# A planner's price for matmuls, halved, in a kernel that weaves a second stream of work between scans

## The chip, the cores and the metric

The kernel runs on one core of a Trainium2 chip. The metric is the device time of one execution in microseconds (us), as the median of several runs.

## The reference

Four images of 96 channels and 64 x 64 pixels go through four layers, all in float32:

- Layer 0 is a state-space layer. After a layer norm, a projection to 192 channels, a 3 x 3 depthwise convolution and SiLU, the 4096 pixels are scanned in four directions (rows, columns, and both backwards) by `h = h * exp(dt * A) + dt * B * x`, `y = sum over 16 states of h * C`, for each of the 192 channels and 16 states. The sum of the directions is normalised, gated with SiLU of a second projection and projected back. An MLP with GELU follows.
- Layer 1 is a group norm, a 3 x 3 convolution and a scan with one state in two directions, gated.
- Layer 2 is a Fourier transform over the pixels with a pointwise complex step and the inverse transform, and an MLP whose operands are rounded to 8-bit floats.
- Layer 3 is a linear attention over 6 heads and a second 8-bit MLP.

## The kernel before

The scans of layer 0 are most of the work. `scan` runs over 4 images x 4 directions x 4 chunks of 1024 pixels x 24 tiles, 1536 tiles in all; a tile is 128 rows (32 channels x 4 states) by 1024 pixels. For each tile:

- GpSimd multiplies u by B into `w` (L745), 2.36 us; there are 9 w buffers.
- ScalarE makes the decay `h = exp(dt * A)` (L144), 1.12 us, with two h buffers, two tiles ahead.
- VectorE scans (L821), 2.35 us.
- The result is multiplied by C, on VectorE (L829, 1.22 us) for two tiles of three or so, on GpSimd (L841, 2.35 us) for the rest.
- The last column is kept as the state for the next chunk (L837 on ScalarE, L834 on GpSimd).
- TensorE sums the states of each two tiles (L767, `py`), three tiles later, and VectorE adds the sums to y (L779, L782).

All the rest is a second piece of work, the **stream**: Python generators whose steps are emitted between the scan's tiles. `front(b)` makes dt, u, B and C of an image (layer norm `pcen`, `pvar`; convolution `pc`; projections `px`, `pd`). `rest(b)` takes an image from the scan's result to the end: `tail` (`pz`, `pca`, `pcb`, `pv`, `po`, `ph`, `pm`), `l1`, `transform`, `middle` and `back`. The four fronts come first in the stream; `rest(b)` is added when image b's last direction begins, and its tail can begin a block of 1024 pixels once the scan has written that block. What is left after the scan is emitted four tasks abreast.

The order on each engine is the order in which the program is emitted. It is set by a planner: a clock for each engine, `now[e]`, and the end of the latest thing that depends on others, `chain[e]`. Each emitted operation adds an estimate to its engine's clock, not before the operands' estimated ends (`spend`, `tick`). For the stream's matmuls the estimate is made in `mm`. The scan's own operations have their fixed prices (sums: 1.5 us for two tiles). Twice a tile, `advance` decides whether the next step of the stream is emitted:

```
late = max(chain["pe"] - 0.5, now["act"], now["pool"] - 6.0, now["pe"] - 2.0) - free
if not put_off and late <= slack:
    step()
```

`free` is VectorE's clock after the scan (and 1.2 us more if VectorE also multiplies), with a slack of 2 us, and the clock 2.4 us on after the tile's end, with a slack of 1 us. VectorE's operations of the stream are not emitted at once: `later` puts them off with the time at which their operands should be there, the largest of the chains of TensorE, ScalarE and GpSimd, and `flush` emits them when VectorE's clock has come to it. While any is put off, no step is let out.

After the scan, steps alternate with a `flush()` that emits everything put off, so that no estimate decides the order there.

Of the kernel before, what the change touches and what calls it, by code (L numbers as in the profile page):

```python
# [11 lines left out]
F32 = mybir.dt.float32  # L12
# [44 lines left out]
def tile_hybrid(ctx: ExitStack, tc: tile.TileContext, I: dict, out: bass.AP):  # L57
# [8 lines left out]
    def tick(e, us, *behind):  # L66
        now[e] = max(now[e], 0.0, *behind) + us
        return now[e]

    def blocks(ap):  # L70
        t = ap.tensor
        if ap.space == DRAM:
            return []
        span = sum(abs(st) * (n - 1) for st, n in list(ap.ap)[1:])
        lo = ap.offset % int(np.prod(t.shape[1:]))
        return [(t.name, q) for q in range(lo // 512, (lo + span) // 512 + 1)]

    def spend(e, us, reads=(), writes=()):
        behind = [chain["dve"]]
        for ap in reads:  # L80
            behind += [done_at.get(q, 0.0) for q in blocks(ap)]
        for ap in writes:
            behind.append(used.get(slot_of.get(ap.tensor.name), 0.0))
        chain[e] = end = tick(e, us, *behind)
        for ap in writes:
            for q in blocks(ap):
                done_at[q] = end
        for ap in (*reads, *writes):
            if ap.tensor.name in slot_of:
                used[slot_of[ap.tensor.name]] = end  # L90

    def size(ap):
        return int(np.prod(ap.shape[1:]))

    def mm(o, lhsT, rhs, side=1, **kw):

        spend("pe", size(rhs) / side * (2.4e-3 if rhs.dtype == F32 else 1.2e-3), (lhsT, rhs), (o,))
        nc.tensor.matmul(o, lhsT=lhsT, rhs=rhs, **kw)  # L98

    dve = nc.vector  # L100
# [158 lines left out]
    def setup():  # L259
# [11 lines left out]
        pool.tensor_scalar(wx[rC], wraw, V("g1", rC), None, ALU.mult)  # L271
        pf = bank("pf")
        mm(pf[C : C + 1, 0:DI], lhsT=V("b1", rC), rhs=wraw, start=True, stop=True)
        dve.tensor_add(wx[C : C + 1], pf[C : C + 1, 0:DI], bi[C : C + 1])

# [18 lines left out]
    def weights():  # L294
# [8 lines left out]
        def task():  # L303
# [14 lines left out]
            pf = bank("pf")  # L318
            b1 = V("b1", rC)
            mm(pf[:, 0:1], lhsT=wraw[:, 0:128], rhs=b1, start=True, stop=True)  # L320
            for h in (lo64, hi64):
                mm(pf[h, 1:2], lhsT=wraw[:, 128:192], rhs=b1, start=True, stop=True)
# [1385 lines left out]
```

## Time and profile before

| | |
|---|---|
| median of 3 runs | 6824.64 us (6809.26 to 6828.71) |
| profiled execution | 6833.64 us, span 6831.9 us |
| instructions in the profile | 52664, of them 15538 matmuls |
| before the first scan | 97 us |
| the scan of 4 images | 97 to 6231 us |
| after the scan | 601 us |
| mean granted TensorE clock | 0.743 |

In the page, PE is TensorE, PEld its weight loads, DVE VectorE, ACT ScalarE and POOL GpSimd. A row of the page gives the line, engine and operation, what is written and read, the shapes, the count, the busy time, the mean of one in ns, and the engine's idle time before it with what ended most of it. A line of helpers stands for many operations: L98 is the matmul in `mm`, L144 the activation in `act`, L148 the copy. The tile names tell them apart.

### The profile page before, as it was taken

To read this page: it belongs to the slowest core of one execution; us is meant where nothing else is said; L and a number is where in the kernel's file an instruction comes from. 1 tells how busy PE (TensorE), PEld (TensorE's weight loads), DVE (VectorE), ACT (ScalarE), POOL (GpSimd) and SP (SyncE) were. 2 spreads that over 40 slices of the span, in tenths; PEclk is the share of its full clock that TensorE was granted. 3 is DMA by queue.
4 is the path that set the end of the run, shared out by engine and by line. 5 is a ranking of instruction groups with operands and counts; after the bars stand their busy time and mean duration, and the time that the engine had idled before them with its cause. 6 is when DMAs were issued, how large, how long until landed. Compare 5 with 4: busy or idle time off the path is not lost. (4 is left out here: it accounts for less than half of the span.)

```text
span 6831.9 us, 52664 instructions
## 1 busy us (share of the span) xinstructions
PE 4673.5 (68%) x15538; PEld 1514.0 (22%) x15538; DVE 5603.1 (82%) x3872; ACT 3731.0 (55%) x5242; POOL 5188.9 (76%) x2732
## 2 busy tenths in 40 slices
PE   6758667676677666666776675657676666576877
PEld 2112111121112124211111142211111332111353
DVE  3888779797789998998899998898999989984413
ACT  3556546666555545665555455566555456553337
POOL 4888879899779788998688898897887889972000
PEclk8768677686778778766777786668777876676987
DMA  5766666767544348444443375454434563442141
GB/s 149 217 194 193 185 180 192 208 207 210 156 132 143 116 136 262 137 146 144 134 151 125 98 262 155 131 158 139 143 128 127 189 209 127 133 144 83 43 125 37
DMA packets 502464, 1050.00 MB, mean 154 GB/s; under 512 B 138448, under 2 KB 252178, under 8 KB 501144
## 3 DMA queue, kind: packets, MB, share of 16 engines
q1 hardware_dynamic: 502176, 1046.63, 49.5%
q8 instruction: 123, 2.02, 0.1%
q14 instruction: 165, 1.35, 0.1%
HBM read 831.15 MB, written 211.09 MB: 153 GB/s over the span
## 5 line engine op out<-in xcount | busy, mean ns | idle before, releaser
L745 POOL TENSOR_TENSOR w<-u,bb 128x1024 f32<-128x1024 f32 x1536 | 3587.5, 2358 | 179.5 <-PE py L767 123.8
L144 ACT ACTIVATE h<-dt,negA 128x1024 f32<-128x1024 f32 x1536 | 1706.8, 1117 | 795.6 <-DVE w L829 429.2
L821 DVE TENSOR_TENSOR_SCAN h<-h,state,w 128x1024 f32<-128x1024 f32 x804 | 1886.8, 2347 | 271.9 <-ACT h L144 202.8
L829 DVE TENSOR_TENSOR w<-h,cc 128x1024 f32<-128x1024 f32 x1072 | 1309.0, 1221 | 56.7 <-DMA cc<-bc_d 18.8
L767 PE MATMUL py<-w,idup 128*32 128x512 f32 x6144 | 1125.3, 805 | 244.1 <-POOL w L841 80.9
L841 POOL TENSOR_TENSOR w<-w,cc 128x1024 f32<-128x1024 f32 x464 | 1092.0, 2353 | 188.3 <-DVE w L821 142.4
L821 DVE TENSOR_TENSOR_SCAN w<-h,state,w 128x1024 f32<-128x1024 f32 x348 | 814.5, 2341 | 50.9 <-ACT h L144 29.2
L837 ACT COPY state<-h 128x1 f32<-128x1 f32 x804 | 127.5, 159 | 1279.4 <-DVE w L829 1278.6
L821 DVE TENSOR_TENSOR_SCAN h<-h,w 128x1024 f32<-128x1024 f32 x268 | 612.9, 2287 | 103.6 <-ACT h L144 73.5
L98 PE MATMUL pc<-xp 97*64 97x512 f32 (+1 forms) x1152 | 400.2, 611 | 12.4 <-DMA xp<-wc_d 7.8
L767 PEld LDWEIGHTS py<-w,idup 128*32 128x32 f32 x6144 | 164.5, 126 | 1057.3 <-issue 597.3
L834 POOL COPY state<-w 128x1 f32<-128x1 f32 x348 | 64.3, 185 | 363.9 <-DVE w L821 363.1
L111 POOL TENSOR_TENSOR u<-dt,xi 128x512 f32<-128x512 f32 x160 | 216.8, 1371 | 156.7 <-ACT dt L144 142.3
L821 DVE TENSOR_TENSOR_SCAN w<-h,w 128x1024 f32<-128x1024 f32 x116 | 264.4, 2279 | 71.9 <-POOL w L745 55.1
L98 PE MATMUL pc<-xp,wc 96*96 96x512 f32 x576 | 275.1, 631 | 25.6 <-ACT u L144 25.6
L98 PE MATMUL pd<-xd,dtw 6*64 6x512 f32 (+1 forms) x512 | 211.4, 983 | 92.8 <-ACT xd L148 59.1
L98 PE MATMUL pcen<-t,cen 96*96 96x512 f32 x192 | 137.5, 853 | 161.3 <-POOL t L1332 78.8
L144 ACT ACT_TABLE_LOAD x176 | 225.8, 1283 | 32.0 <-PE pd L98 18.1
L136 ACT ACT_TABLE_LOAD x174 | 223.2, 1283 | 3.8 <-PEq L1698 0.7
L98 PEld LDWEIGHTS pc<-xp 97*64 97x64 f32 (+1 forms) x1152 | 149.9, 167 | 270.2 <-issue 239.4
L98 PE MATMUL po<-hq,q 128*96 128x512 fp8e5 x192 | 88.7, 586 | 163.0 <-POOL hq L1320 132.1
L98 PE MATMUL pvar<-sq,avg 96*96 96x512 f32 x256 | 168.9, 801 | 45.3 <-ACT sq L144 45.3
(242 smaller groups left out, 6330.8 us busy)
## 6 DMA issues: line engine op xcount, KB each, us to landing
u<-u_d SPq DMA_DIRECT2D x384, 512.0 KB
dt<-dt_d SPq DMA_DIRECT2D x384, 512.0 KB
bb<-bc_d SPq DMA_DIRECT2D x256, 512.0 KB
cc<-bc_d SPq DMA_DIRECT2D x256, 512.0 KB
dt_d<-dt SPq DMA_DIRECT2D x128, 256.0 KB
u_d<-u SPq DMA_DIRECT2D x128, 256.0 KB
f_d<-fo SPq DMA_DIRECT2D x64, 384.0 KB
a<-f_d SPq DMA_DIRECT2D x64, 384.0 KB
```

Source lines behind the costliest of these rows:

```text
L98: nc.tensor.matmul(o, lhsT=lhsT, rhs=rhs, **kw)
L111: aside(0.2 + size(o) * 2.1e-3, o, a, b).tensor_mul(o, a, b)
L136: nc.scalar.preload_act_table_set("natural_log_exp_and_others")
L144: nc.scalar.activation(o, i, func, **kw)
L745: pool.tensor_mul(w, us[ci, 2 * p + a], bbs[ci, g])
L767: nc.tensor.matmul(o, lhsT=idup, rhs=v, **flags)
L821: dve.tensor_tensor_scan(o[:, r], h[:, r], w[:, r], state if step else 0.0, ALU.mult, ALU.add)
L829: dve.tensor_mul(w, o, cc)
L834: pool.tensor_copy(state, o[:, last : last + 1])
L837: nc.scalar.copy(state, o[:, last : last + 1])
L841: pool.tensor_mul(w, o, cc)
```

## The change

The two factors of the estimate in `mm`, in us for each column of the moving operand: from 2.4e-3 to 1.2e-3 for float32, and from 1.2e-3 to 0.9e-3 for the other type that it is called with (8-bit floats). `side` is the number of such matmuls that are taken to run side by side. The operations stay the same; the order in which the stream's steps stand among the scan's tiles is worked out anew.

```diff
     def mm(o, lhsT, rhs, side=1, **kw):
 
-        spend("pe", size(rhs) / side * (2.4e-3 if rhs.dtype == F32 else 1.2e-3), (lhsT, rhs), (o,))
+        spend("pe", size(rhs) / side * (1.2e-3 if rhs.dtype == F32 else 0.9e-3), (lhsT, rhs), (o,))
         nc.tensor.matmul(o, lhsT=lhsT, rhs=rhs, **kw)
```

## The prediction

> **What bounds the kernel now.** I read the page's busy line first, then a table of windows (one for each image's scan, cut at the 1st, 385th, 769th and 1153rd scan instruction), then the waits, then single stretches of the timeline.
>
> ```profile
> span 6831.9 us, 52664 instructions
> ...
> PE 4673.5 (68%) x15538; PEld 1514.0 (22%) x15538; DVE 5603.1 (82%) x3872; ACT 3731.0 (55%) x5242; POOL 5188.9 (76%) x2732
> ...
> L98 PE MATMUL pc<-xp 97*64 97x512 f32 (+1 forms) x1152 | 400.2, 611 | 12.4 <-DMA xp<-wc_d 7.8
> ```
>
> Busy time, in the same order of engines as on the page, then the granted clock and the DMA share:
>
> ```profile
> 97.00:1641.00 1544.00, 1105.32 (x3438) 297.23 (x3439) 1301.14 (x787) 895.51 (x1197) 1325.45 (x713) 0.73 0.66 198
> 1641.00:3158.00 1517.00, 996.67 (x3399) 316.51 (x3397) 1369.41 (x930) 839.07 (x1173) 1294.82 (x675) 0.73 0.49 155
> 3158.00:4707.00 1549.00, 1047.23 (x3487) 332.36 (x3488) 1383.24 (x954) 854.14 (x1201) 1284.77 (x664) 0.74 0.48 152
> 4707.00:6231.00 1524.00, 1023.52 (x3476) 328.67 (x3474) 1378.74 (x948) 852.62 (x1195) 1266.71 (x656) 0.74 0.45 143
> 6231.00:6831.90 600.90, 457.14 (x1622) 224.00 (x1622) 166.63 (x244) 265.69 (x443) 1.55 (x8) 0.80 0.27 76
> ```
>
> The scan takes 6134 us of the span, and in it VectorE is busy 1301.14 + 1369.41 + 1383.24 + 1378.74 = 5432.53 us. It does the same instructions whatever the order, so the only thing that a new order can change there is VectorE's 701 us of idle time (11%). The last 601 us hold the rest of image 3, where every step is emitted with a flush of all put-off work and no estimate is asked: I give the change nothing there, within 15 us either way for how much of image 3's tail is already done.
>
> The waits in the scan (who <- whom: us in total, times, longest):
>
> ```profile
> ACT sbb L144 <- PE pcb L98: 62.4, 14, 7.0
> ACT y L148 <- PE py L98: 60.1, 20, 8.2
> ACT xd L148 <- PE px L98: 56.1, 14, 14.2
> ACT pvar L144 <- PE pvar L98: 52.6, 74, 2.9
> ACT sq L144 <- PE pcen L98: 50.0, 39, 7.8
> ```
>
> With the smaller rows of the same list, ScalarE stands 534 us in 392 waits for a matmul of the stream. VectorE's own rows: 396 us ended by ScalarE (decay, state), 131 us by the sums of line 767, 106 us by GpSimd. GpSimd in turn stands 124 us for line 767, which frees its w buffers. The tie between them is seen in one stretch of image 1's scan, in which the rest of image 0 runs:
>
> ```profile
> 1824.14 1.97 PE L98 MATMUL pcb<-ya,cenr 128*64 128x512 f32 x2
> 1826.04 1.97 PE L98 MATMUL pcb<-yb,cenr 64*64 64x512 f32 x2
> 1827.93 1.93 PE L767 MATMUL py<-w,idup 128*32 128x512 f32 x8
> 1828.04 0.60 ACT L144 ACTIVATE sbb<-pcb 128x512 f32<-128x512 f32 x1 [6.99 <-PE pcb L98]
> 1830.72 2.36 DVE L821 TENSOR_TENSOR_SCAN h<-h,state,w 128x1024 f32<-128x1024 f32 x1 [7.24 <-ACT state L837]
> ```
>
> ScalarE was given sbb too early, stood 6.99 us for TensorE, had the next decay and the state copy behind it, and VectorE lost 7.24 us.
>
> **What an estimate should be.** The six-call steps of pc call mm 36 times a task, 16 tasks: 576 calls. The page counts 1152 instructions. So one float32 mm is two instructions, and the 611 ns of the pc row is half a call. The back-to-back pace is in the timeline after the scan:
>
> ```profile
> 6337.55 61.98 PE L98 MATMUL pc<-xp,wc 96*96 96x512 f32 x144
> ```
>
> 61.98/144 = 0.43 us an instruction, 0.86 us a call, when TensorE is kept busy. The two pcb lines above show 1.97 us for two instructions, one call, when it is not. The old estimate for 512 columns is 512 x 2.4e-3 = 1.23 us, between the two. The new one, 0.61 us, is 0.7 of the fastest call and under a third of the slowest. For a conv step of six calls (5.2 us at 0.86 us a call) the old estimate, 7.4 us, was 2.2 us long and the new, 3.7 us, is 1.5 us short: a draw. For a two-call step of a layer norm or a projection (four instructions of 0.43 to 0.98 us: 1.7 to 3.9 us) the old 2.46 us lay inside and the new 1.23 us lies below.
>
> **What the Trainium skill says.** "TensorE: Matmul & The Clock Gate", part 1 (What's actually happening): the array runs at half rate until it has been busy for a window of about 3.4 us. The trace agrees: 0.43 against 0.98 us an instruction, mean granted clock 0.73 to 0.74 in the scan. The same page, Engine queue depths: ScalarE, VectorE and GpSimd take their queues strictly in order. The sbb stretch shows that for ScalarE. "Perfetto Trace Analysis" (Identifying the Most-Contended Engine) warns that matmul busy time misleads because matmuls are pipelined; hence the spacing is used above, not the 611 ns.
>
> **The change part by part.** No instruction is added or removed; the f8 matmuls' estimate goes from 0.61 to 0.46 us (0.75 times), float32 to a half. What moves is where the stream's steps stand between the scan's tiles.
>
> *The gate.* A step is let out when chain pe - 0.5, act, pool - 6 and pe - 2 are all within 2 (or 1) us of VectorE's clock. With a half as long estimate the pe terms, and act through what it reads, fall by 1.23 us for a two-call step and up to 3.7 us for a conv step. There are two chances a tile, 1.2 to 2.4 us apart, so the fall means about one chance earlier, where pe was what refused. Nothing waits for the stream to be ahead: the tails of images 1 and 2 start (first pz by its tile view at 3163 and 4596 us) while or just after the scan of that image ends (3158, 4707 us). So being earlier buys nothing in itself, and it leaves stretches with no step at the end of each image.
>
> *ScalarE.* An activation that reads a matmul now stands in its queue earlier. I let half of the 392 waits grow by the cut of a two-call step: 196 x 1.23 = 241 us. What of it reaches VectorE: against 534 us of such waits stand 396 us of VectorE's waits for ScalarE, which table loads and long activations cause too; I take 0.4. That makes +96 us. Bounds: 0.1 (the decay runs two tiles ahead and covers most) to 0.75 (the two sums' ratio): +24 to +180 us.
>
> *Behind it on other queues.* The stream's matmuls also stand earlier before the sums of line 767, and whatever TensorE has too much of delays py, the w buffers and GpSimd (131 + 106 us of VectorE's idle now). The put-off VectorE steps fall due by the same clocks and may then wait on VectorE itself (now 13 us, xr <- po). The stream's DMAs go with their steps on SP's one queue; image 0's scan, where all fronts run, moves 198 GB/s at share 0.66, and closer steps would raise it. Together I price these at +10 us, with -20 to +60 us as bounds.
>
> *Given back.* Closer matmuls may keep the clock up. If that takes a fifth off the 534 us, at the same 0.4, it is -43 us; bounds 0 and -110 us (half of it).
>
> Sum: 96 + 10 - 43 = **+63 us**. The profiled execution took 6833.64 us (span 6831.9 and 1.7 around it), 9.0 us over the median of 6824.64: 6897 us in its terms, **6888 us** as a median.
>
> **The rivals.** *Faster: the clock.* Steps let out closer together keep TensorE at full rate, and the waits shrink: in the tail at 3252 us, where two pcb instructions take 1.07 us in place of 1.97, sbb waits 3.4 us in place of 7.0. If 534 us of ScalarE's waits fall by a third, 178 us, at the same 0.4, that is -71 us: 6754 us. For it: clock 0.73 in the scan, so about half the time at half rate. Against it: tails and layer norms are chains, and a chain's matmuls are apart however early they are issued. It decides if the scan's mean clock rises over 0.80.
>
> *Nothing to be seen.* Other terms hold the step: in image 0 GpSimd's clock, later the put-off VectorE work, which refuses a step by itself. Then the steps hardly move: 6825 us.
>
> *It does not do what it says.* The trace's time may have been read per instruction, not per call: then the new estimate is no nearer to the chip than the old. That is part of the first case, and gives its sign.
>
> **How the numbers follow.** Slower as worked out: 0.50; its own range is 6845 us, where a loss can first be told, to 6995 us (180 for ScalarE, 10, -43 and some 20 us of chance). Faster through the clock: 0.37. No change: 0.13. Which stall meets which tile is partly chance: alike stretches now differ (VectorE idle in the four images' scans: 243, 148, 166, 145 us). The range over all cases goes down to 6730 us, the faster case and 25 us of that chance. A difference under 0.3% (20 us) is what this measurement cannot tell from none.
>
> **What would show it.** Right: VectorE's idle time in the scan over 730 us, ScalarE's waits for the stream's matmuls over 600 us in sum (now 534), fronts ended before 1640 us and the first pz before 1734 us, the last 601 us unchanged, the instruction counts the same. Wrong: those waits at or under 534 us, or the granted clock over 0.80. Then the estimate was too long for the chip, however many instructions a call has.

## Result: slower by 5.9%

The changed kernel takes 7224.32 us (7209.95 to 7243.31), the kernel before 6826.68 us beside it: a ratio of 1.059 [1.0558, 1.0621], 398 us (the bracket is a 95% interval, here and below). The forecast had the direction, to which it gave one chance in two; its +63 us is a sixth of the size, and the result lies above its range.

The page after, in the lines that answer to those of before:

```profile
span 7228.6 us, 52744 instructions
...
PE 4828.1 (67%) x15538; PEld 1532.5 (21%) x15538; DVE 5612.2 (78%) x3872; ACT 3749.8 (52%) x5245; POOL 5187.5 (72%) x2732
```

The matmuls (15538) and VectorE's instructions (3872) are the same in number; ScalarE loads its function table three times more (353 for 350). VectorE's busy time grew by 9 us. The windows by image, in the same columns as before:

```profile
98.00:1868.00 1770.00, 1275.73 (x3694) 338.59 (x3694) 1333.16 (x832) 987.71 (x1321) 1351.94 (x729) 0.72 0.62 182
1868.00:3446.00 1578.00, 1010.01 (x3371) 317.59 (x3374) 1370.52 (x931) 823.77 (x1149) 1274.70 (x661) 0.71 0.44 143
3446.00:5026.00 1580.00, 1013.75 (x3368) 316.43 (x3366) 1369.29 (x929) 823.44 (x1148) 1274.80 (x660) 0.70 0.45 143
5026.00:6622.00 1596.00, 1022.78 (x3368) 319.29 (x3368) 1368.58 (x929) 823.81 (x1148) 1268.51 (x658) 0.70 0.43 137
6622.00:7228.60 606.60, 462.03 (x1622) 225.12 (x1622) 166.47 (x243) 266.60 (x443) 1.55 (x8) 0.79 0.26 75
```

The part after the scan is as it was (607 against 601 us). The loss is in the scan, and there in VectorE's idle time: 6524 - 5442 = 1082 us, against 701 us. Image 0's scan, where the fronts run, is 226 us longer, the other three 61, 31 and 72 us. Some 32 us of image 0's share are no loss but VectorE's own work, which now falls into it (1333 us busy in place of 1301); its idle time there grew by 194 us, that of the others by 186 us together. The granted clock in the scan went down, from between 0.73 and 0.74 to between 0.70 and 0.72. The stream did get ahead: the last front matmul ends at 1532 us in place of 1696, and the first pz is at 1564 us in place of 1734.

The waits of the scan after (who <- whom: total, times, longest):

```profile
DVE h L821 <- ACT h L144: 394.9, 131, 18.4
...
POOL w L745 <- PE py L767: 357.9, 95, 13.9
...
DVE h L821 <- ACT state L837: 116.3, 58, 16.3
...
DVE w L821 <- ACT h L144: 104.7, 32, 11.0
```

The same four rows before:

```profile
DVE h L821 <- ACT h L144: 276.2, 144, 13.5
...
POOL w L745 <- PE py L767: 123.8, 57, 6.3
...
DVE h L821 <- ACT state L837: 44.2, 26, 7.2
...
DVE w L821 <- ACT h L144: 33.0, 17, 7.1
```

And from ScalarE's own list after:

```profile
ACT sbb L144 <- PE pcb L98: 86.8, 15, 7.0
ACT xi L144 <- PE pc L98: 79.4, 17, 8.9
...
ACT u L144 <- PE pc L98: 34.0, 15, 3.7
```

The two rows that name pc were not in the list of before at all. Taken over all rows, ScalarE stood 868 us for matmuls of the stream (552 before, the smallest rows included), VectorE's idle time ended by ScalarE went from 418 to 702 us, and GpSimd's waits for the sums from 124 to 358 us. Sorted by what ended it, VectorE's 381 us of new idle time are: ScalarE +284 us, TensorE +110 us (the sums +62, matmuls of the stream that VectorE reads itself +48), DMA +23 us, GpSimd -38 us. So GpSimd's longer waits for the sums do not show as waits of VectorE for GpSimd. In the 358 us for which GpSimd waited for the sums, TensorE was idle for only some 16 us (the two engines' instructions laid over each other): the sums stood behind other matmuls, not behind one that waited for its operand.

One stretch of the timeline, the conv steps of one task in image 0's scan, shows how the queues hang together:

```profile
540.69 7.96 PE L98 MATMUL pc<-xp 97*64 97x512 f32 x36
540.86 4.69 POOL L745 TENSOR_TENSOR w<-u,bb 128x1024 f32<-128x1024 f32 x2 [1.66 <-PE py L767]
...
548.58 1.07 PE L767 MATMUL py<-w,idup 128*32 128x512 f32 x8
548.70 0.69 ACT L144 ACTIVATE xi<-pc,vec 128x512 f32<-128x512 f32 x1 [8.21 <-PE pc L98]
...
549.74 2.35 POOL L745 TENSOR_TENSOR w<-u,bb 128x1024 f32<-128x1024 f32 x1 [4.19 <-PE py L767]
...
550.70 1.12 ACT L144 ACTIVATE h<-dt,negA 128x1024 f32<-128x1024 f32 x1
...
551.92 2.29 DVE L821 TENSOR_TENSOR_SCAN w<-h,w 128x1024 f32<-128x1024 f32 x1 [8.45 <-ACT h L144]
```

The 18 calls of pc2 stand in one piece between two sums. They take 7.96 us. The new estimate for them, with side 2, is 18 x 0.61 / 2 = 5.5 us, the old one 11 us. ScalarE came to SiLU 8.2 us too early, the decay stood behind it, the sums behind the matmuls, GpSimd behind the sums, and VectorE lost 8.45 us.

### The profile page after: what moved, and what is told of

The parts are those of the page before. It is cut to its first block, busy times and chain, and to the rows that moved or that the text cites. A ratio compares the mean times of both kernels' runs of the same rounds, so it can differ in the third digit from the quotient of the medians.

```text
span 7228.6 us, 52744 instructions
## 1 busy us (share of the span) xinstructions
PE 4828.1 (67%) x15538; PEld 1532.5 (21%) x15538; DVE 5612.2 (78%) x3872; ACT 3749.8 (52%) x5245; POOL 5187.5 (72%) x2732
## 5 line engine op out<-in xcount | busy, mean ns | idle before, releaser
L767 PE MATMUL py<-w,idup 128*32 128x512 f32 x6144 | 1278.5, 854 | 727.3 <-DVE y L782 268.2
L829 DVE TENSOR_TENSOR w<-h,cc 128x1024 f32<-128x1024 f32 x1072 | 1309.6, 1222 | 85.5 <-DMA cc<-bc_d 44.5
L767 PEld LDWEIGHTS py<-w,idup 128*32 128x32 f32 x6144 | 181.3, 129 | 1720.6 <-issue 602.3
L98 PE MATMUL pc<-xp,wc 96*96 96x512 f32 x576 | 252.5, 595 | 0.0
```

Source lines behind the costliest of these rows:

```text
L767: nc.tensor.matmul(o, lhsT=idup, rhs=v, **flags)
L829: dve.tensor_mul(w, o, cc)
```

## Experiments

All times are medians; each ratio is to the kernel before, measured on the same chip, with its interval. "Image 0", "1 to 3" and "after" are the lengths of image 0's scan, of the other three together, and of what follows the last scan, cut at the same scan instructions of each run's one profile (the last cut lies one or two us later than in the windows above). One profile stands for each run, so a few us of these lengths are chance. The code cuts show only the lines that matter; those of e5 to e8, e11 and e12 are written from the pair of factors or the line that they replace.

| run | us | ratio | image 0 | 1 to 3 | after |
|---|---|---|---|---|---|
| before | 6827 | | 1544 | 4590 | 600 |
| after | 7224 | 1.059 [1.0558, 1.0621] | 1770 | 4756 | 604 |
| e1 8-bit only | 6812 | 0.9987 [0.9975, 0.9999] | 1546 | 4577 | 581 |
| e2 fronts new | 6951 | 1.0194 [1.0164, 1.0224] | 1747 | 4501 | 592 |
| e3 rest new | 7095 | 1.0406 [1.0364, 1.0447] | 1542 | 4832 | 601 |
| e4 tight gate | 6993 | 1.0254 [1.0217, 1.0291] | 1632 | 4664 | 599 |
| e5 long runs new | 7026 | 1.0270 [1.0237, 1.0304] | 1762 | 4587 | 602 |
| e6 short runs new | 7001 | 1.0237 [1.0209, 1.0265] | 1539 | 4756 | 601 |
| e7 1.7e-3 | 7043 | 1.0295 [1.0263, 1.0327] | 1706 | 4616 | 601 |
| e8 put-off later | 7186 | 1.0507 [1.0478, 1.0535] | 1782 | 4701 | 600 |
| e9 before, freed | 6682 | 0.9779 [0.9746, 0.9812] | 1520 | 4511 | 555 |
| e10 after, freed | 6928 | 1.0125 [1.0079, 1.0170] | 1671 | 4615 | 557 |
| e11 2.9e-3 | 7011 | 1.0261 [1.0225, 1.0297] | 1538 | 4448 | 912 |
| e12 by kind | 6896 | 1.0094 [1.0060, 1.0128] | 1528 | 4451 | 817 |
| e13 long runs, freed | 6779 | 0.9933 [0.9910, 0.9956] | 1626 | 4497 | 555 |
| e14 short runs, freed | 6830 | 1.0014 [1.0002, 1.0026] | 1520 | 4648 | 556 |
| e15 before, thinned | 6821 | 0.9992 [0.9976, 1.0007] | 1542 | 4581 | 600 |
| e16 after, thinned | 7116 | 1.0432 [1.0411, 1.0453] | 1672 | 4754 | 600 |
| e17 after, both | 6911 | 1.0120 [1.0081, 1.0159] | 1636 | 4631 | 554 |
| e18 both, put-off later | 6895 | 1.0098 [1.0063, 1.0133] | 1640 | 4617 | 553 |

**Which part of the change.** My theory was ScalarE's queue, entered through the gate; the rivals were VectorE's put-off work and a crowded TensorE.

```diff
# e1
-(1.2e-3 if rhs.dtype == F32 else 0.9e-3)
+(2.4e-3 if rhs.dtype == F32 else 0.9e-3)
# e2; e3 has the two pairs exchanged
+Now.fronts = stream[0].__name__ == "front"        # in step()
-(1.2e-3 if rhs.dtype == F32 else 0.9e-3)
+((1.2e-3 if rhs.dtype == F32 else 0.9e-3) if Now.fronts else (2.4e-3 if rhs.dtype == F32 else 1.2e-3))
# e4
-FIRST, SECOND = 2, 1
+FIRST, SECOND = 0.8, -0.2
```

> Only the 8-bit factor is shortened (1.2e-3 to 0.9e-3); float32 stays at 2.4e-3. All theories: the 8-bit matmuls are single instructions and are few (336 calls of the stream a chip run, 0.15 us each), so under a tenth of the loss: 6800 to 6870 us. If it gives over 6950 us, the loss is not that of the float32 estimates.

> The new factors only while a front is at the head of the stream (image 0's scan), the old ones for everything else. The windows of the two profiles put 226 us of the loss in image 0's scan and 164 us in the other three. If the loss is made where the estimate is short: 7020 to 7080 us, with image 0's scan near 1770 us and the other three near 1517, 1549 and 1524 us. If it comes from the tails starting as soon as their blocks are written (which early fronts bring about too): image 1 to 3 longer as well, 7150 us or more.

> The complement: new factors for the rest of each image, old ones for the fronts. If the two parts add up: 6970 to 7020 us, image 0's scan near its 1544 us. If early fronts were needed for the loss in the later images: 6850 us or less.

> The new factors with the gate's slack cut by 1.2 us at both places (2 and 1 become 0.8 and -0.2), so that a step must wait for about the time that was taken off a two-call step; the due times of put-off VectorE work stay early. Gate theory (ScalarE gets activations before their matmuls can be done): most of the loss comes back, 6850 to 6980 us, and ScalarE's waits for the stream's matmuls fall from 868 us to under 650. Put-off theory (VectorE's own steps are due too early): 7150 us or more, since their due times are unchanged.

The 8-bit factor (384 matmuls in the trace of before) is not the cause: 0.9987, if anything a gain of some 10 us. The fronts alone cost 1.9%, the rest 4.1%, together 6.0%: they add up to the whole 5.9%. Neither came out as expected. e2 is below its range (7020 to 7080 us): image 0's scan is nearly as long as in after (1747 against 1770 us), but the later scans are shorter than before (4501 against 4590 us), perhaps because each rest begins earlier when the fronts are done early and then spreads over a whole image; no run shows that by itself. e3 is above its range (6970 to 7020 us), most of all in image 1 (1678 us in place of 1517), in which what remains of image 0's rest and the beginning of image 1's are both run at the new prices.

e4 gives 232 of the 398 us back with the due times of put-off work as they were, and ScalarE's waits for the stream are down from 868 to 650 us, both just short of what was expected. So more than half of the loss goes when the gate alone is tightened. What a tighter gate would do to the kernel before was not run.

**Long and short runs.**

```diff
# e5, with long = name of o in ("pc", "pc2", "ph", "pm", "pf")
-(2.4e-3 if rhs.dtype == F32 else 1.2e-3)
+((1.2e-3 if long else 2.4e-3) if rhs.dtype == F32 else 1.2e-3)
# e6
+((2.4e-3 if long else 1.2e-3) if rhs.dtype == F32 else 0.9e-3)
# e7
+(1.7e-3 if rhs.dtype == F32 else 1.2e-3)
# e8, with the new pair
-put_off.append((fn, us, max(chain[e] for e in ("pe", "act", "pool"))))
+put_off.append((fn, us, 1.2 + max(chain[e] for e in ("pe", "act", "pool"))))
```

> Half as long estimates only for the float32 matmuls of the long runs (pc, pc2, ph, pm, pf: three and more calls a step, convolutions, GELU MLP, transform); all others as before. The prediction called a conv step a draw (2.2 us too long before, 1.5 us too short after): by that 6800 to 6870 us. Rival, from image 0's rows (ScalarE for xi <- pc 0 before, 79 us after; GpSimd for py 0 before, 125 us after): conv steps follow each other, five to a task, so their shortfall adds up to 5 to 9 us before SiLU reads; by that 6950 to 7080 us, with most of the loss in image 0's scan.

> The complement: the new factors for everything but the long runs (layer norms, projections, tail, inverse, 8-bit MLPs). By the prediction (two-call steps fall below the fastest measured) this is most of the loss: 7100 to 7230 us. By the rival it is the smaller part: 6950 to 7050 us.

> float32 at 1.7e-3 a column: 0.87 us for 512 columns, the pace of a call in a long run at full rate; 8-bit at its old 1.2e-3. If an estimate at the fastest pace is enough: 6780 to 6850 us. If what counts is the pace at half rate and the waits behind the sums, which the estimate has to stand in for: about 0.58 of the way from the old to the new, 6950 to 7080 us.

> The new factors, but put-off VectorE work falls due 1.2 us later than the chains say; while it is put off no step is let out. If early VectorE work is a main cause (put-off rows rose from 21 to 69 us): 7100 to 7170 us with those rows back near 21 us. If it is not: the gate is also held longer by it, so a gain up to 100 us may come with those rows little changed; 7130 to 7230 us.

Both halves cost (2.7% and 2.4%, in sum 5.1%; 192 and 167 us over the kernel before beside them), and in different places. The long runs' loss is nearly all in image 0's scan, the short runs' in the later images:

```profile
98.00:1861.00 1763.00, 1285.69 (x3697) 344.52 (x3700) 1334.73 (x833) 989.27 (x1322) 1353.49 (x729) 0.71 0.62 183
1861.00:6449.00 4588.00, 2979.55 (x10107) 950.65 (x10104) 4109.56 (x2787) 2464.88 (x3444) 3819.11 (x1976) 0.72 0.46 146
```

These are the windows of e5; the same two of e6:

```profile
98.00:1638.00 1540.00, 1092.03 (x3433) 297.45 (x3436) 1299.76 (x788) 892.87 (x1192) 1320.74 (x710) 0.74 0.66 197
1638.00:6396.00 4758.00, 3159.42 (x10374) 985.59 (x10368) 4146.41 (x2832) 2560.91 (x3572) 3852.48 (x1997) 0.72 0.46 145
```

The long runs, with the conv step that the prediction called a draw, are half of the loss. The two halves also reach VectorE differently. In e5 its idle time grew by 205 us: ended by the sums +150, by ScalarE +118, by GpSimd -59. In e6 it grew by 149 us: ended by ScalarE +189, by the stream's matmuls +49, by the sums -34. e7 shows that the back-to-back pace of a call is not enough either: 3.0% slower with 0.87 us for a call. e8 gives 38 us back, with VectorE's waits for the stream's matmuls down from 69 to 38 us, so early put-off work is a small part.

**ScalarE's reads taken away.** In e9 and e10 each activation or copy of the stream that reads PSUM (the memory that the matmuls write, in banks) and writes SBUF (where the other tiles lie) reads a constant instead; the planner still sees the old operand, so that the order stays. The data after such a read are left out, and the banks are no longer held by it. The rsqrt pairs (a logarithm and an exponential, which work in place in PSUM) stay.

```diff
+            i = apart(o, i)                    # in act, for the stream's activations
...
+    def apart(o, i):
+        if i.space != PSUM or o.space == PSUM:
+            return i
+        v = eps[0 : i.shape[0]]
+        return (v if len(i.shape) == 2 else v[:, :, None]).to_broadcast(list(i.shape))
...
-        nc.scalar.copy(o, i)
+        nc.scalar.copy(o, apart(o, i))
```

> The kernel before with its order and planner untouched, but every activation or copy of the stream that reads PSUM and writes SBUF reads a constant instead (so the images' data beyond that point are left out, and TensorE's banks are no longer held by those reads). ScalarE then never stands for those matmuls. Theory of ScalarE's queue: its 552 us of such waits go to under 150 us (those of the in-place rsqrt stay), and VectorE's idle falls by about as much as the waits it was charged with: 6500 to 6720 us.

> The same with the new factors: the order of the kernel after, ScalarE's reads of PSUM taken away. ScalarE's queue: the two orders come together, within 80 us of the run before this one. Rival, TensorE's own backlog (sums late, w buffers and y late, with ScalarE a bystander): 250 to 400 us stay between them.

It is worth 145 us in the order of before and 297 us in that of after, so 152 us of the 398 go with ScalarE's reads, and 245 us stay. That is close to the rival's number (250 to 400 us), but it does not show that ScalarE is a bystander in the rest, because ScalarE's queue was not emptied. In e9 it still stands 187 us for TensorE, where under 150 were expected, and 73 us for DMA; in e10 319 and 182 us. The largest of these rows in e10 are a pair of the rsqrt, and a copy that overwrites a tile whose store is not yet done:

```profile
ACT pvar L145 <- PE pvar L98: 155.1, 85, 9.2
ACT o L155 <- DMA g_d<-o: 75.9, 33, 6.5
```

In e9 these two are 92 and 6 us. Of the 246 us that VectorE is idle longer in e10's scan than in e9's, ScalarE ended 139, TensorE 83 and DMA 25 us. So the 152 us, in which the banks set free earlier have a share that no run parts, are not all that ScalarE's queue carries; the rest is not divided by these two runs.

> Long runs re-priced as in the run with only them, and ScalarE's PSUM reads replaced by a constant as in the two runs before (the images' data are left out from there). Crowding of TensorE by long runs: the sums are late whoever reads the banks, so most of the 192 us that the long runs cost stay over the freed order of before: 6830 to 6890 us, nearly all in image 0's scan. ScalarE's queue: 6680 to 6740 us.

> The complement with ScalarE's reads taken away. If the short runs cost through ScalarE's queue: most of their 167 us go, 6680 to 6740 us. If they cost through VectorE's put-off work or TensorE: 6800 us or more.

The same with one half re-priced each. Over e9, the long runs cost 97 us (192 us with the reads) and the short runs 148 us (167 us with them). e13 lies between its two ranges, e14 in its upper one. What stays is not of the same kind.

In e13 ScalarE stands for TensorE no longer than in e9 (174 against 187 us), and VectorE's idle time ended by ScalarE fell from 319 to 256 us. The loss comes by the sums: VectorE's waits for them grew from 186 to 279 us, those for GpSimd from 51 to 103 us, GpSimd's for the sums from 82 to 209 us. VectorE's rows of e9, then of e13:

```profile
DVE y L786 <- PE py L774: 107.7, 26, 19.4
DVE y L789 <- PE py L774: 78.7, 13, 15.5
```

```profile
DVE y L789 <- PE py L774: 149.5, 22, 17.1
...
DVE y L786 <- PE py L774: 129.9, 31, 10.4
```

So 97 us of what the long runs cost do not need ScalarE's waits, and come by the sums. In e14 it is the other way round: VectorE waits less for the sums (152 us), and 124 of its 133 us of new idle time are ended by ScalarE, which stands 274 us for TensorE (187 in e9) and 159 us for DMA (73 in e9). The short runs' loss does not go with the reads, but it still comes through ScalarE's queue, at reads and buffers that the experiment left in place. In e14 GpSimd waits 151 us for TensorE (90 in e9), and VectorE 54 us for the stream's matmuls directly (24 in e9).

**TensorE uncrowded.** In e15 and e16 two of each nine matmuls of the fronts' convolutions are emitted, and the planner is charged for nine; the other seven taps are left out of the result.

```diff
-                            start=(kh == kw == 0), stop=(kh == kw == 2),
+                            start=(kh == kw == 0), stop=(kh == kw == 2), thin=kh + kw not in (0, 4),
...
+        if not thin:                          # in mm, after spend
+            nc.tensor.matmul(o, lhsT=lhsT, rhs=rhs, **kw)
```

> The order of before with two of each nine matmuls of the fronts' convolutions emitted and the planner still charged for all nine (the convolution's other seven taps are left out). In before, conv steps had room, so little changes: image 0's scan 1480 to 1545 us, in all 6760 to 6830 us.

> The order of after with the same taps left out. Crowding of TensorE by the fronts' long runs: image 0's scan comes back from 1770 us to within 80 us of the thinned order of before, and about 170 us of the 398 go: 6990 to 7080 us. If the loss in image 0 is from elsewhere (DMA, px and pd, tail 0 starting in it): 7150 us or more.

In the order of before, 840 matmul instructions fewer in image 0's scan (2598 in place of 3438) change nothing (1542 us): there TensorE had the room that the planner thought it had. In the order of after they bring image 0's scan from 1770 to 1672 us:

```profile
94.00:1767.00 1673.00, 1046.83 (x2854) 234.91 (x2854) 1331.85 (x832) 986.76 (x1322) 1351.41 (x730) 0.66 0.65 193
```

In all 108 of the 398 us go, where 170 were expected, and image 0's scan stays 130 us over e15's, where at most 80 were. That the convolutions hold TensorE is thus real, and explains some half of the 194 us of idle time that image 0 gained. It costs more by ScalarE, which stands for the convolutions' result, than by the sums: VectorE's idle time there falls from 277 to 205 us where ScalarE ends it for the scan, and from 53 to 31 us where the sums do.

> The order of after with both taken away: seven of nine taps of the fronts' convolutions left out, and ScalarE's PSUM reads replaced by a constant. If the two costs add up: 7224 - 153 - 104 - the 143 us that the freed reads give in any order, about 6820 us, 140 us over the freed order of before (6682). If they are the same stalls: about 6900 us.

> As before, and put-off VectorE work due 1.2 us later (which by itself gave 38 us and changes the order). If that adds up too: 6780 us. If the put-off work waited only because its ScalarE part was late: no change, 6820 us or what the run before this one gives.

With the convolutions thinned and ScalarE's reads taken away (e17), and put-off work due 1.2 us later besides (e18), the savings do not add up. e17 takes 6911 us, which cannot be told from the freed order alone (6928 us): most of what the thinned convolutions gave back in e16 was the SiLU that stands for them, the same stall. 229 us over e9 stay, half in image 0, half in the others. Later put-off work makes no difference that can be told (6895 us). VectorE's idle time in the scan is 831 us in e17 and 602 in e9, and of the 229 us between them ScalarE ended 171. e17's waits beside e9's, over the whole scan: ScalarE for the in-place rsqrt and the like 320 us (187) and for DMA 180 us (73), GpSimd for the sums 265 us (82), VectorE for the stream's matmuls 64 us (24) and for a C tile still being loaded 44 us (18). No run takes one of these away alone, so how the 229 us are shared between their causes stays open.

**Longer estimates.**

```diff
# e11
-(2.4e-3 if rhs.dtype == F32 else 1.2e-3)
+(2.9e-3 if rhs.dtype == F32 else 1.2e-3)
# e12, with by_kind = 1.5 for pcen, 1.8 pz, 1.66 pca, 1.45 pcb, 3.1 py, 1.3 pkv, pd, pcy, 1.47 pB, pC, else 1
+(2.4e-3 * by_kind if rhs.dtype == F32 else 0.9e-3)
```

> float32 at 2.9e-3 a column (1.48 us a call), 8-bit at 1.2e-3. On the line of the three points so far (1.2e-3: 7224 us, 1.7e-3: 7043, 2.4e-3: 6826) the loss goes on falling, to 6700 us; if the old value was where the stream just keeps up, the fronts and rests fall behind the scan and what is left over runs after it: 6850 to 7000 us with the part after the last scan over 650 us. Likeliest 6800 us.

> The old 2.4e-3 times a factor from the trace of before for the kinds whose steps took TensorE longer than their estimate (pcen 1.5, pz 1.8, pca 1.66, pcb 1.45, inverse py 3.1, pkv, pd and pcy 1.3, pB and pC 1.47), 8-bit at 0.9e-3; the long runs keep 2.4e-3. If the estimate has to cover what the step takes with its waits: faster than before, 6650 to 6780 us. If the old value is as good as any: 6800 to 6850 us.

Both are slower, and for the opposite reason: too little of the stream is done when the scans end. e11 is just above the range of its second case and shows that case's sign, the longer part after the last scan; e12 is above both of its ranges. The windows of e11 in and after the scan:

```profile
97.00:6086.00 5989.00, 3928.30 (x13215) 1197.97 (x13216) 5374.02 (x3531) 3253.47 (x4458) 5131.68 (x2674) 0.73 0.53 164
6086.00:6998.60 912.60, 716.10 (x2206) 313.73 (x2204) 247.74 (x357) 447.55 (x734) 6.85 (x12) 0.79 0.22 63
```

The scan is 146 us shorter than before (6135 us), but the stream has fallen behind: image 2's last store is issued at 6301 us, after the last scan, and 313 us are added at the end, where nothing covers them. Over the four estimates 2.9, 2.4, 1.7 and 1.2e-3 the scan takes 5989, 6135, 6324 and 6526 us, always more with a shorter estimate, and the part after it 912, 600, 601 and 604 us. With the old value the stream still keeps up: in before, image 2's last store is issued at 6005 us, 226 us before the last scan ends. Values between 1.7 and 2.4e-3, or between 2.4 and 2.9e-3, were not run. e12 shows the same turn (a scan of 5982 us, and 817 us after it), although its prices come from what each kind of step took in the trace. No run that leaves the work whole clearly beats the kernel before; e1's 0.9987 is at the edge of its interval.

## Why the prediction was right in direction and wrong in size

- **Two instructions a call, so the new figure is short: right.** e7 goes further: even 0.87 us a call is short. What is missing there (the sums ahead in TensorE's queue, the clock, the wait for an operand) was not taken apart. The two paces that the prediction sets side by side, 0.43 and 0.98 us an instruction, are not of a kind: one is the spacing in a long run, the other half the length of one call. Like calls of pcb take 1.07 and 1.97 us.
- **"A draw" for the conv steps: wrong.** It compared one step with its estimate. At the new price the steps stand back to back (18 calls in one piece in the stretch above, 7.96 us against 5.5), and ScalarE stands 113 us for pc where it stood for none. e5: 192 us by itself.
- **"About one chance earlier": too small a picture.** It shifts each step by the cut of one two-call step. The fronts were done 164 us earlier.
- **ScalarE's waits: the sum nearly right, in part by luck.** Forecast 241 us more, measured 316 us more (552 to 868 us). The forecast let half of the waits grow by 1.23 us; in the trace there are a quarter more waits (398 to 508), each 0.3 us longer in the mean, and 113 of the 316 us are the two rows of pc, which were called a draw.
- **ScalarE's term, +96 us with a bound of +180: too small.** Taking reads away gave VectorE 99 us for 365 us of waits in the order of before (0.27) and 234 us for 549 in that of after (0.43), so 0.4 was fair for a wait that goes. But 152 us went with the reads, and by the trace's account the term is 284 us, over its bound.
- **"Behind it on other queues", +10 us with a bound of +60: the step that failed.** The profile of before showed the path (GpSimd's 124 us for the sums, VectorE's 131 us for y), and the text named it, but gave it a price without a working. e13 shows 97 us on this path for the long runs alone, with ScalarE's waits no longer than before; in the changed kernel VectorE's idle time ended by TensorE itself grew by 110 us. The 245 us that stay without ScalarE's reads are not all on it, since much of them still passes through ScalarE.
- **"Given back", -43 us: it did not come.** The clock went down, from 0.743 to 0.716 over the execution, and the faster case that rested on it fell with it. Whether the lower clock added to the loss was not tested.
- **The sum.** Forecast 96 + 10 - 43 = 63 us. By the trace's account of VectorE's idle time it is 284 us for ScalarE, some 95 us for all others, and nothing given back. This account names only what ended a wait last; how much of the 284 us would have stayed with an empty ScalarE queue is open.
- **Being earlier buys nothing: right** for the changed kernel (601 to 607 us after the scan). The other side of it, that a later stream costs at once, was not seen and is what e11 measured.
- **The part after the scan, the numbers of matmuls and of VectorE's instructions, the fronts' end, the first pz, ScalarE's waits over 600 us and VectorE's idle time over 730 us** came as foretold.
- **Put-off work and DMA**: 38 us by e8, nothing that can be told by e18, and the wait for C's row went from 18.8 to 44.5 us. Small, as priced.

## What to carry to other kernels

An estimate that decides an order on in-order queues is not a measurement of an instruction. Count first how many instructions one call makes; but here neither the pace of a call (e7) nor the time that each kind of step took (e12) did better than the tuned value. Ask of such a planner both what a shorter and what a longer estimate would break: here a shorter one stalls the queues, a longer one leaves work uncovered at the end, and the tuned value sits between. When pricing an earlier step, price every queue that it enters, the sums behind it included, by the waits that the profile already lists for that queue. And when an experiment takes one kind of wait away, look at what the engine waits for then: here ScalarE's queue stalled at the next operand, and the time that stayed was still partly its own.

## What was not expected of the hardware

Seven of nine matmuls of the fronts' convolutions could be left out of the order of before with no change (0.9992 [0.9976, 1.0007]), though TensorE's busy time in image 0's scan fell from 1105 to 919 us. And leaving them out lowered the clock that was granted there, from 0.73 to 0.65. The matmuls that stayed took longer where they had run quickly; the sums, before and with the taps left out:

```profile
L767 PE MATMUL py<-w,idup 128*32 128x512 f32 x1528 | 301.9, 834 | 129.6 <-DVE y L779 47.5 <-POOL w L841 35.6 <-DVE w L829 24.0
L768 PE MATMUL py<-w,idup 128*32 128x512 f32 x1536 | 359.2, 931 | 314.7 <-DVE y L780 99.0 <-POOL w L842 90.6 <-DVE y L783 74.0
```

The two convolution shapes went from 626 and 598 to 854 and 846 ns an instruction, while px and pd, with means of 0.9 to 1.1 us, stayed within 3%. So the busy time of the convolutions fell by some 245 us (377 to 131 us), but TensorE's by 186 us only: the sums took back 57 us of what the experiment removed.
